# One cross-attention kernel, a second written-out order: the 2,366 steps rearranged, and the engine chosen anew where there is a choice

## The chip, the cores and the metric

The kernel runs on one core of one Trainium2 chip. Its engines run side by side, each through a list of instructions of its own, strictly in order: TensorE (PE, matrix products; loading its weights is listed apart as PEld), VectorE (DVE), ScalarE (ACT), GpSimd (POOL) and SyncE (SP, which here issues nearly all transfers). An instruction waits on semaphores for what it reads, and everything behind it on the same engine waits with it. The metric is device time in microseconds (us) of one execution; smaller is better.

## What is computed

Two batches of 2,048 tokens with 640 features (`x`) attend, in 8 heads of 80 features, to 124 text tokens, and the result gets an adapter term that is built from 4 further tokens (`ca`). Cut to what matters:

```python
query = x @ Wq;  keyt = enc @ Wk;  valt = enc @ Wv
hs = mha(query, keyt, valt)                            # softmax over 124 tokens
ca_q1 = einsum('btc,th->bch', ca, Wq_ca)[:, indices]   # 384 rows, repeated over 2048
ca_hs1 = mha(ca_q1, x, x)                              # softmax over 2048 tokens
ca_hs2 = mha(ca_hs1 @ Wq, ca @ Wk_ca, ca @ Wv_ca)      # softmax over 4 tokens
out = (hs + ca_hs2) @ Wout + b_out + x
```

All data are float32.

## The kernel before

**An order written out by hand of a planner.** The kernel consists of small tasks, Python generators that yield steps (`Do`: an engine or a choice of engines, what must be known before, which room is taken and freed). Nothing in the kernel decides the order. The string `ORDER` lists 2,366 entries; `Desk.run` takes them one by one, and each entry lets the task of that number do its next step. So the order of the entries of one engine is the order of that engine's instructions. A letter behind the number names the engine where a step has a choice (a ACT, v DVE, g POOL, n none); without a letter the first engine of the step's list is taken. Tasks are numbered as they are begun. The first 37 numbers are fixed (36 is the adapter of batch 0), then come the groups of the 16 units, then numbers that are given out as tasks start others.

**What the tasks do.** x comes in blocks of 512 tokens (`x_load`, turned by DVE), and each gives queries (`queries_fast`: a product by a scheme with 7 products of halves in place of 8, so with sums of halves of x and of Wq ahead of it, its strips of 32 columns in four parts of the array). The adapter of a batch (`adapter`) makes 24 blocks of scores of which DVE takes maxima (`mx`), then 24 blocks of which ACT takes exponentials (`ea`), each followed by a product that sums over tokens (`contract`, tile `acc`). After the last comes a chain that passes through all engines (`second`): `divide` (DVE), `less` (DVE, tiles `s2f`, `m`, `p`), an exponential (ACT), `share` (DVE, `r`, `p2t`), a product `pt_p` (PE, with `rows` made on POOL by `rows_of_tokens`), a copy, and a transfer to HBM from which each unit of the batch reads its part.

**Units.** The 32 tiles of 128 tokens are taken in 16 units of two. `text_scores` makes scores (`sc`), `softmax` takes maxima (DVE), exponentials (ACT), a scaling (POOL or DVE) and a turn (DVE); the result goes to HBM (`kept`) and comes back with keys along the partitions (`pT`). Then comes the hidden product (`ph`) and the output product (`po`). Seven units (0 to 4, 6 and 7) use sums of halves again (`text_out_fast`, four chains of products; between two products on one bank DVE adds the first to the rows of x: task `sums_chain`). The other nine (`text_out`) split both factors into a high part `top`, a rest `low` and a `mix` of both, and make 15 products in a faster type for each of four quarters (`out_part`). For that, Wout is split once for its five chunks (`wout_part`: `top`, `low`, a scaling, `mix`, a scaling). The parts `low` lie in a tile that is free only after both `contract` tasks of batch 1, and no `out_part` can start before all five chunks are done.

**Names and lines.** All matmuls run at line 221, nearly all other instructions at line 236, transfers at line 246. `Desk.run` is at line 181, `second` and `rows_of_tokens` stand below line 1640, `sums_chain` and `out_part` below line 2140, and `stored` writes a row of the output once its last sum is there.

Of the kernel before, what the change touches and what calls it, by code (L numbers as in the profile page):

```python
# [8 lines left out]
F32 = mybir.dt.float32  # L9
# [5 lines left out]
P = 128  # L15
# [52 lines left out]
class Desk:  # L68
# [7 lines left out]
    2 4 4 0 2 36 0 0 2 0 0 2 0 0 2 0 0 2 0 0 2 2 124 2 4 2 0 128a 0 2 0 6 6 6 2 125 4 6 130a 126 4 131a 127 4 4  # L76
    132a 6 133v 2 3 4 6 3a 2 15 3 6 3a 15 15 3 6 3v 3 7 7 8 8 7 8 11 7 7 15 0 8 135a 0 134a 7 5 8 7 7 15 9 7
    137a 6 1 138a 136v 14 8 12 15 7 7 7 139a 7 7 141v 140v 7 142a 9 15 143a 8 144 15 9 8 8 36 8 145 5 15 15 8 8
    9 10 8 9 5 146 5 9 147 15 14 36 15 15 148 6 9 9 9 14 14 14 14 9 14 9 14g 129 152a 151v 149a 12 150v 15 153 6
    6 9 36 14 129 15 14 36 16 14g 11 9 129 129 101 36 155 155 12 155 155 11a 36 157 11 9 12 9 156a 9 155 12 158  # L80
    158 159v 158 158 158 9 36 160 162v 18 12 36 163a 12 13 36 117 123 158 17 154 158 158 158 154 154 39 161 123
    17 117v 161 165g 154 161 117v 171 175 17 161 166g 161 164 18 164 164 17 18 117g 36 164 117g 154 154 164 117g
    164 161 18 176a 164 36 164g 161 16 36 18 18 167g 171 177 16 164 16 16 16 18 36 178a 117v 117 18 43 16 36 16g
    171 181 161 117g 18 18 180 164 168g 180 36 182a 16 17 180 117g 179 180 36 179 16 171 183 16g 174 185 184a 18
    180 18 180 18 36 172 186 36 174 18 17 17 179 18 179 174 188 170 187 187 19 20 21 161 21 187 187 172 192 187
    20 189 190 21 187 36 43 36 179 179 21 173 203 203 203 191 191 36 193 191 173 204 169 103 203 191 180 36 180g
    203 191 19 21 203 21 194g 180 36 19 200 209 20 21 195g 19 36 19 191 21 39 102 210a 191 19 21 21 36 19 191
    212 200 213 211 19g 205 211 212 17 196g 20 214a 203 19 212 197g 211 212 36 200 215 211 212 180 203g 201 212
    191 20 19 212 21 216a 21 19g 21 36 20 20 21 212g 211 211 21 206 217 217 36 22 23 24 24 202 24 200 218 217
    217 24 206 222 219a 203 217 36 22 223 24 217 203 36 24 47 22 22 22 208 228 226 202 202 22 24 207 229 24 44  # L90
    226 226 226 212 226 36 22 208 36 226 220 22g 24 207 230 202 224 208 232 199 198 105 202 231 212 226 36 23 24
    233 234g 47 36 20 226g 240 245 23 24 24 202 202 202 23 241 246a 22 241 241 40 241 36 235v 23 241 226 237g 22
    241 36 240 247 226 236g 154 23 23 248a 24 51 24 249 249 202 249 249 249 221 221 249 179 36 241 250 241g 221
    240 255 221 250 250 221 36 22g 244 257 256a 250 221 241 240 259 258a 250 36 241 221 244 154 36 250 55 260
    250 48 250g 36 221 261 242 261 261 24 261 36 25 26 27 27 244 262 239 261 27 261 243 26 264g 250 27 265g 36
    261 243 271 263 267g 27 36 242 273 238 107 179 250 266g 51 104 251 27 274 261g 36 272 270 279 26 36 23 253
    277 280a 27 227 275 270 281 227 275 275 154 261 275 179 275 277 283 282v 261 275 36 284a 278 285 36 221 225
    55 286v 179 225 275 227 275g 225 36 287 225 278 27 287 287 227 36 287 27 27 270 288 287 225 287 275 278 290
    269 276 289 275 287 36 36 36 36 287g 227 227 270 292 291 36 225 225 225 225 276 294 293 252 252 27 25 52 36
    295 287 252 154 252 59 25 252 25 211 26 296 296 296 252 27 296 27 296 59 106 27 296 27 36 28 29 29 30 287 26  # L100
    298 252 252 36g 298 252 296 299v 298 254 254 305 310 29 211 298 30 297 300g 298 36 30 56 36 311v 26 26 268
    26 109 296g 36 25 30 305 314 313 301g 312 30 36 315a 254 312 36 254 254 305 316 25 298 312 36 298 296 298g
    312 36 308 296 297 306 211 317a 312 30 313 36 313 313 312 25 36 305 320 30 308 322 321v 313 312 30 313 36 63
    302g 36 30 30 312 254 326 227 254 312 326 312 326 323 326 36 297 309 327 326 298 326 36 298 67 211 328 25 30
    297 30 227 312 254 36 329 309 36 30 329 60 30 312 329 30 312 309 330 304 326 329 31 32 326g 254 36 297 32
    331 312 227 36 318 326 324 31 329 312 227 329 326 36 319 319 31 312 10 36 319 67 33 33 33 31 340 31 312 36
    339 312 36 339 29 329 329g 339 312 339 36 332g 33 329 29 36 333g 33 312 339 312 340 334g 29 29 339 33 36 341
# [142 lines left out]
def kernel(  # L250
# [42 lines left out]
    desk = Desk(tc)  # L293
# [827 lines left out]
    def sums_of_wq():  # L1121
# [1245 lines left out]
```

## Time and profile before

| | |
|---|---|
| device time, median of 3 runs | 566.38 us |
| lowest and highest of them | 563.15 and 566.64 us |
| span of the profiled execution | 562.1 us |
| busy: PE, DVE, ACT, POOL | 549.2, 402.2, 276.3, 208.1 us |
| moved by transfers | 101.38 MB |

The span runs from the first to the last instruction; what an execution takes around it has no row of its own, and the three timed runs lie 1.1 to 4.5 us above the span. Durations in the following are those of the one profiled execution. A busy PE says that a product is under way, not that the next one could not have come sooner.

### The profile page before, as it was taken

How to read it: one execution, taken by the hardware profiler on the slowest of the kernel's cores; microseconds unless marked ns; L12 is line 12 of the kernel's file. 1: busy time of each engine (PE TensorE's matmuls, PEld its weight loads, DVE VectorE, ACT ScalarE, POOL GpSimd, SP SyncE). 2: the span in 40 equal slices, each digit the busy share in tenths (PEclk: the TensorE clock that was granted, in tenths of full speed). 3: DMA queues.
4: the chain of work that ended last, by engine and by line, in shares of the span. 5: the costliest groups of instructions: out<-in, count | busy, mean ns of one | idle time of the engine just before them, and what ended most of it. 6: DMA issues, size and time to landing. Idle time of an engine off the chain costs nothing.

```text
span 562.1 us, 17332 instructions
## 1 busy us (share of the span) xinstructions
PE 549.2 (98%) x7338; PEld 337.8 (60%) x7338; DVE 402.2 (72%) x621; ACT 276.3 (49%) x752; POOL 208.1 (37%) x206
## 2 busy tenths in 40 slices
PE   9999999999999999999999999999999899999997
PEld 8563455556555655455365445455554477989796
DVE  2457999999996564589999998655735886449542
ACT  3122645445338898886524524589878432111200
POOL 7002625344424522013559364512424830441040
PEclk9999999999999999999999999999999989999999
DMA  8994759774876899446558895859865367977533
GB/s 258 244 175 121 163 123 166 163 159 142 170 199 155 183 251 180 136 160 176 177 126 247 226 232 133 255 149 254 244 172 177 74 124 215 264 215 195 160 123 129
DMA packets 151549, 101.38 MB, mean 180 GB/s; under 512 B 86476, under 2 KB 130012, under 8 KB 151472
## 3 DMA queue, kind: packets, MB, share of 16 engines
q1 hardware_dynamic: 150704, 99.88, 69.5%
q8 instruction: 58, 0.95, 0.8%
q0 software_dynamic: 768, 0.40, 0.4%
q14 instruction: 19, 0.16, 0.1%
HBM read 61.34 MB, written 38.90 MB: 178 GB/s over the span
## 4 chain that ended last, share of the span: by engine, by line
PE 82%; DVE 7%; DMA 5%; ACT 2%; issue 2%; SPq 1%; DVEq 0%; ACTq 0%
PE po L221 23%; PE pq L221 23%; PE acc L221 7%; PE sc L221 6%; PE s L221 6%; PE ph L221 5%; PE pq_first L221 3%; PE pyz L221 3%; DVE mx L236 2%; ACT p L236 1%; DMA bias<-in_L_xattn_b_out_dram 1%; PE pk L221 1%; PE unread L225 1%; ACT ea L236 1%; PE pv L221 1%
## 5 line engine op out<-in xcount | busy, mean ns | idle before, releaser
L236 DVE TENSOR_REDUCE mx<-s 128x4 f32<-128x2048 f32 x48 | 109.2, 2275 | 2.9 <-PE s L221 2.8
L236 POOL TENSOR_TENSOR p<-p,r 128x992 f32<-128x992 f32 x29 | 53.8, 1856 | 141.1 <-DVE r L236 135.0
L236 ACT ACTIVATE ea<-s 128x2048 f32<-128x2048 f32 x48 | 90.4, 1884 | 25.6 <-PE s L221 25.3
L236 ACT ACTIVATE p<-sc,m 128x124 f32<-128x124 f32 x256 | 89.5, 374 | 25.7 <-DVE m L236 25.7
L236 ACT ACTIVATION_READ_ACCUMULATOR p<-sc,m 128x1 f32 x256 | 55.5, 217 | 0.0
L221 PE MATMUL pq<-xt,wq_sb 128*32 128x256 f32 x896 | 54.3, 381 | 0.6 <-DVE q L236 0.6
L236 DVE TENSOR_REDUCE m<-sc 128x4 f32<-128x496 f32 x64 | 40.6, 662 | 13.9 <-PE sc L221 13.7
L221 PE MATMUL acc<-ea,y_sb 128*32 128x384 f32 (+2 forms) x768 | 50.1, 383 | 0.0
L221 PE MATMUL ph<-pT,vpad 128*32 128x256 f32 x768 | 45.8, 380 | 0.8 <-DMA out_dram<-x_more 0.3
L236 DVE STREAM_TRANSPOSE eb<-p 128x1024 f32<-128x1024 f32 x32 | 39.5, 1233 | 4.5 <-POOL p L236 3.3
L221 PEld LDWEIGHTS pq<-xt,wq_sb 128*32 128x32 f32 x896 | 27.5, 110 | 22.9 <-issue 5.5
L221 PEld LDWEIGHTS sc<-kmain,q 64*128 64x128 f32 x512 | 31.8, 187 | 11.6 <-issue 8.4
L221 PE MATMUL pq<-xt,wq 128*32 128x512 f32 x320 | 38.8, 595 | 0.0
L221 PE MATMUL po<-wout_sums,hs 128*32 128x320 f32 x448 | 35.4, 438 | 3.5 <-DVE x_more L236 2.9
L221 PE MATMUL sc<-kmain,q 64*128 64x124 f32 x512 | 37.5, 283 | 0.1
L221 PE MATMUL po<-wout_sb,hs 128*32 128x320 f32 (+1 forms) x452 | 36.4, 434 | 0.7 <-DVE prod L236 0.6
L221 PE MATMUL po<-wout_low,ks 128*128 128x320 f32 x204 | 35.7, 308 | 0.0
L221 PEld LDWEIGHTS ph<-pT,vpad 128*32 128x32 f32 x768 | 24.4, 110 | 18.6 <-issue 2.6
L236 POOL TENSOR_TENSOR last_rows<-last_rows,bias 128x640 f32<-128x640 f32 x10 | 17.0, 1697 | 44.7 <-DMA last_rows<-in_x_dram 44.7
L221 PE MATMUL po<-wout_top,ks 128*128 128x320 f32 x180 | 32.5, 311 | 0.0
L221 PEld LDWEIGHTS acc<-ea,y_sb 128*32 128x32 f32 x768 | 21.1, 109 | 17.3 <-issue 8.6
L221 PEld LDWEIGHTS po<-wout_low,ks 128*128 128x128 f32 x204 | 31.3, 188 | 0.0
(232 smaller groups left out, 951.4 us busy)
## 6 DMA issues: line engine op xcount, KB each, us to landing
kept<-eb SPq DMA_DIRECT2D x32, 512.0 KB
pT<-kept SPq DMA_DIRECT2D x48, 256.0 KB
landing<-away SPq DMA_DIRECT2D x60, 128.0 KB
xi<-in_x_dram SPq DMA_DIRECT2D x28, 256.0 KB
x_more<-in_x_dram SPq DMA_DIRECT2D x17, 320.0 KB
out_dram<-x_more SPq DMA_DIRECT2D x16, 320.0 KB
last_rows<-in_x_dram SPq DMA_DIRECT2D x15, 320.0 KB
out_dram<-last_rows SPq DMA_DIRECT2D x14, 320.0 KB
```

Of the source, the lines that this page charges most:

```text
L221: self.pin(self.nc.tensor.matmul(out[strip], lhsT[:, strip], rhs, **kw))
L225: self.pin(self.nc.tensor.matmul(out, zeros, zeros, start=True, stop=True))
L236: return lambda *args, **kw: self.pin(getattr(engine, what)(*args, **kw))
```

## The change

It is all in the order, in the choice of engines, and in the bookkeeping that lets the order be made: a few rooms (tiles or banks that tasks share) are now freed or added by the step itself and no longer by the line behind it, the two steps of the hidden parts' `mix` became a helper that offers the same engines, and the stores of the output are tasks that exist from the start of a unit and wait for marks, where before the last sum started them. What is computed, and with which instructions, stays the same; of `BY_SUMS`, the tiles and the transfers nothing is changed. The entries were laid out anew with every transfer taken to land later than was estimated for what waits for it.

Both lists have 2,366 entries. Of the lists, the lines around the end of the second adapter and the last line stand here; with entries counted from 0, the first lines shown begin with entry 1965 before and 1947 after. In the part before, 515 is the second `contract` task of batch 1, 541 is `second`, 542 `rows_of_tokens`, 536, 537, 538, 543 and 544 are the five `wout_part` tasks. In the part after, the same are 542, 560, 561, and 543, 546, 549, 562, 563; 556 to 559 are the four chains of unit 4, 540 the end of a chain of unit 6, 129 the scores of unit 15, 70 unit 5, whose parts are 565, 566 and 567 and whose four output quarters are 568 to 571.

```diff
     ORDER = """
...
-    515 515 450 544v 544a 538v 538a 536v 536a 543g 543a 537v 99 116 120 451 538v 538a 543v 543a 541 533 533 60
-    84 11 84 84 84 537a 537v 541 541 541 60 547a 547 542 534 60 548a 548 548v 548 544g 544a 532 532 60 80 80
-    549a 549 549v 549 60 80 80 80 533 542 542 541 541a 541 84 119 92 80 88 88 88 88 88 88 547v 547 536g 536a 535
...
-    626 636 72 640 638 638 637 639 637 641 72 627 642 640 599 643 639 644 620 92 620 645
...
+    542 106 338 561 542 556 561 154 154 562 542 561 556 551v 556 542 542 480 546v 542 562 129 148 556 546 542 560 557
+    561 152 70 481 562 563 549v 560 560 560 70 556 565 70 561 549 540 76 563v 565 563 70 543v 566 563 565a 560 566 100
+    100 567 70 543 556 558 567 560 557 567a 562v 560 563 100 546v 557 562 549v 546 100 100 567v 549 559 543v 566 543
+    565v 556 64 558 152 566 569 540 151 100 556 106 547 557 568 564 564 564 564 571 564 100 112 112 112 112 112 47 112
...
+    120 626 118 641 635 642 626 119 132 125 108 640 88 642 643 90 633 130 640 89 633 131
     """
...
-        yield Do("NONE", lambda: None, ["late"], marks=["wq room"])
+        yield Do("NONE", lambda: None, ["late"], grows=[(halves[1], 1)], marks=["wq room"])
...
-        halves[1].grow(1)
...
-                op = yield Do("PE", scores, [("cop", b)], needs=[(quad, 1), (eas, 1)])
+                st = pieces(v)[-1][0]
+                ends_ = j == 1 and 512 * (v + 1) == CAD * (st + 1) and st % 4 == 3
+                op = yield Do(
+                    "PE", scores, [("cop", b)], needs=[(quad, 1), (eas, 1)],
+                    frees=(lambda st=st: [(zops, room_of["zop", b, st // 4])]) if ends_ else (),
+                )
...
-                    zops.give(room_of["zop", b, st // 4])
+                    late["ps_"]=0
...
+    def mixing(mix, top, low, after, marks):
+
+        def first():
+            if desk.engine == "ACT":
+                desk.a_activation(mix(), raw(low()), AF.Identity, scale=UP)
+            else:
+                mixed(mix(), raw(top()), raw(low()))
+
+        op = yield Do(("DVE", "ACT"), first, after)
+
+        def second():
+            if op.ran == "ACT":
+                minus(mix(), raw(top()), raw(mix()))
+
+        yield Do(("NONE", "POOL", "DVE"), second, marks=marks)
...
-    def stored(m, k, u, added):
+    def stored(m, k):
 
         b, st = tiles(m)[k]
...
+        for u in (2,) if m < UNITS - 1 else (0, 1):
+
+            def store(u=u):
+                cols = slice(*spans[u])
+                dma(out[b, st * P : (st + 1) * P, cols], xr_of[m][k][0][:, cols])
...
+            yield Do(
+                "SP", store, added,
+                frees=lambda: [(rows, xr_of[m][k][1])] if u == 2 else [],
+            )
```

The last entries tell which unit ends: before, entry 2365 is the store of unit 13, one of whole rows; after, it is the second store of unit 15 (131), one of half rows.

More of the change, by code (lines that the diff above doesn't have):

```diff
@@ L81 @@
[L81 to L95, printed above, removed]
@@ L2188, in add @@
                     desk.v_tensor_tensor(t, t, po[:, :HALF], ALU.add)
-                op = yield Do("DVE", add, [op.at], frees=[(banks, s)] if end else [])
+                op = yield Do(
+                    "DVE", add, [op.at], frees=[(banks, s)] if end else [], marks=[("added", m, i, n, k)],
+                )
                 at = [op.at]
-                key = (m, i, 2)
-                ends.setdefault(key, []).append(op.at)
-                if len(ends[key]) == 4:
-                    yield Fork(stored(*key, ends[key]))
         for n, steps in enumerate(chains):
@@ L2237, in hidden_parts @@
         )
-        def scaled():
-            if desk.engine == "ACT":
-                desk.a_activation(cols("mix"), cols("low", True), AF.Identity, scale=UP)
-            else:
-                mixed(cols("mix"), cols("top", True), cols("low", True))
-        op = yield Do(("DVE", "ACT"), scaled)
-        both = op.ran == "ACT"
-        yield Do(
-            ADDS if both else "NONE", lambda: both and minus(cols("mix"), cols("top", True), cols("mix", True)),
-            marks=[("hs mix", m, c0)],
-        )
+        yield from mixing(lambda: cols("mix"), lambda: cols("top"), lambda: cols("low"), [("hs low", m, c0)], [("hs mix", m, c0)])
     def out_part(m, i, u, hs):
@@ L2275, in add @@
             desk.v_scalar_tensor_tensor(t, po[:, :HALF], 1.0 + DOWN, t, ALU.mult, ALU.add)
-        op = yield Do("DVE", add, [op.at, ("xr", m, i)], frees=[(banks, s)])
-        key = (m, i, 2 if m < UNITS - 1 else u)
-        ends.setdefault(key, []).append(op.at)
-        if len(ends[key]) == (2 if key[2] == 2 else 1):
-            yield Fork(stored(*key, ends[key]))
-    ends = {}
+        yield Do("DVE", add, [op.at, ("xr", m, i)], frees=[(banks, s)], marks=[("added", m, i, u)])
     spans = (0, HALF), (HALF, H), (0, H)
-    def stored(m, k, u, added):
+    def stored(m, k):
         b, st = tiles(m)[k]
-        t, i, _ = xr_of[m][k]
-        cols = slice(*spans[u])
-        yield Do(
-            "SP", lambda: dma(out[b, st * P : (st + 1) * P, cols], t[:, cols]), added,
-            frees=[(rows, i)] if u == 2 else [],
-        )
+        for u in (2,) if m < UNITS - 1 else (0, 1):
+            def store(u=u):
+                cols = slice(*spans[u])
+                dma(out[b, st * P : (st + 1) * P, cols], xr_of[m][k][0][:, cols])
+            if m in BY_SUMS:
+                parts = (((0, 0), (0, 2), (2, 0), (3, 0)), ((0, 1), (0, 3), (1, 0), (1, 1)))[k]
+                added = [("added", m, k, *part) for part in parts]
+            else:
+                added = [("added", m, k, v) for v in ((0, 1) if u == 2 else (u,))]
+            yield Do(
+                "SP", store, added,
+                frees=lambda: [(rows, xr_of[m][k][1])] if u == 2 else [],
+            )
     blocks = [(b, sb) for b in range(B) for sb in range(NSB)]
@@ L2304, in text @@
         yield Fork(probabilities(m))
+        for k in range(2):
+            yield Fork(stored(m, k))
     begin = desk.begin
```

152 lines of the change are left out of this document (79 added, 73 removed).

## The prediction, made before the changed kernel was run

> **What bounds the kernel now.** I read the page's totals first, then the slices, then the waits of PE, then windows around the one place where the slices show a hole.
>
> ```profile
> span 562.1 us, 17332 instructions
> ...
> PE 549.2 (98%) x7338; PEld 337.8 (60%) x7338; DVE 402.2 (72%) x621; ACT 276.3 (49%) x752; POOL 208.1 (37%) x206
> ...
> PE   9999999999999999999999999999999899999997
> ...
> PEclk9999999999999999999999999999999989999999
> ...
> PE 82%; DVE 7%; DMA 5%; ACT 2%; issue 2%; SPq 1%; DVEq 0%; ACTq 0%
> ```
>
> PE is busy for 549.2 of 562.1 us, so its open idle time is 12.9 us in all. The chain that ended last gives only 82% to PE, which looks like more room. It isn't: where the chain names DVE or a transfer, the slices above still have PE at 9, so PE worked on something else while the step that came next was released. The waits show what PE itself lost, and to whom:
>
> ```profile
> PE po L221 <- DVE x_more L236: 2.9, 1, 2.9
> PE unread L225 <- DVE zeros L236: 1.1, 1, 1.1
> PE s L221 <- DVE mx L236: 1.1, 2, 0.8
> PE pt_p L221 <- DVE ks L236: 0.5, 1, 0.5
> PE ph L221 <- DMA out_dram<-x_more: 0.3, 1, 0.3
> ```
>
> The largest wait, 2.9 us, is on DVE and happens once. The one wait of PE that is put down to a transfer is 0.3 us. So the idea that the list is laid out by, a margin for late transfers, insures against something that costs this execution next to nothing in open waits. What a new order can win or lose is decided elsewhere: in the hole of slice 32. Its windows (columns: busy time of PE, PEld, DVE, ACT, POOL, then the granted clock) and its instructions:
>
> ```profile
> 438.98:456.64 17.66, 14.32 (x197) 7.51 (x196) 17.20 (x28) 8.38 (x15) 14.57 (x13) 0.90 0.32 65
> ...
> 446.00:447.00 1.00, 0.96 (x20) 0.31 (x12) 1.00 (x1) 0.68 (x1) 0.93 (x2) 1.00 0.00 0
> 447.00:448.00 1.00, 0.00 (x0) 0.00 (x0) 1.00 (x3) 0.76 (x2) 1.00 (x2) 1.00 0.20 12
> 448.00:449.00 1.00, 0.00 (x0) 0.00 (x0) 0.96 (x3) 0.60 (x1) 0.93 (x2) 1.00 0.94 174
> 449.00:450.00 1.00, 0.18 (x4) 0.16 (x8) 0.97 (x4) 0.60 (x2) 0.93 (x2) 1.00 0.67 174
> ...
> 451.00:452.00 1.00, 1.00 (x12) 0.21 (x4) 0.96 (x2) 0.55 (x2) 1.00 (x1) 0.50 1.05 231
> ```
>
> ```profile
> 438.43 0.55 PE L229 MATMUL pt_acc<-ident,accs 128*128 128x128 f32 x3
> ...
> 439.29 0.46 DVE L236 TENSOR_TENSOR prod<-pt_acc,r 128x288 f32<-128x288 f32 x1
> 439.66 5.51 DVE L236 TENSOR_TENSOR wout_low<-wout_sb,wout_top 128x640 fp32r<-128x640 f32 x4
> ...
> 440.40 1.28 PE L221 MATMUL po<-wout_sums,hs 128*32 128x320 f32 x16
> ...
> 441.50 1.05 PE L221 MATMUL ph<-pT,vpad 128*32 128x256 f32 x16
> ...
> 445.10 2.10 DVE L236 TENSOR_TENSOR wout_mix<-wout_top,wout_low 128x640 fp32r<-128x640 f32 x2
> ...
> 447.13 1.66 DVE L236 TENSOR_REDUCE s2f<-prod 128x24 f32<-128x192 f32 x3
> ...
> 449.29 0.47 DVE L236 TENSOR_TENSOR x_more<-x_more,po 128x320 f32<-128x320 f32 x1
> ...
> 449.82 1.66 PE L221 MATMUL po<-wout_sums,hs 128*32 128x320 f32 x16 [2.85 <-DVE x_more L236]
> ...
> 450.68 0.24 DVE L236 TENSOR_REDUCE r<-p 128x24 f32<-128x96 f32 x1
> ...
> 451.30 1.07 DVE L236 TENSOR_TENSOR p2t<-p,r 128x96 f32<-128x96 f32 x1
> 452.21 1.27 DVE L236 TENSOR_TENSOR ks<-ph,ks 128x512 fp32r<-128x512 f32 x2
> ...
> 453.04 1.52 PE L221 MATMUL pt_p<-rows,p2t 128*32 128x512 f32 x12 [0.49 <-DVE ks L236]
> ...
> 456.64 1.00 PE L221 MATMUL po<-wout_top,ks 128*128 128x320 f32 x5
> ```
>
> The last product of the adapter of batch 1 (`pt_acc`) ends at 438.98. From there to the first product of `out_part` at 456.64, DVE is busy for 17.20 of 17.66 us: it is the bound of this stretch, and PE has too little else to do. DVE takes four `wout_low` and two `wout_mix` first, then `s2f` and the rest of `second`, and only then the `x_more` sum that PE's next step waits for. PE is idle for 17.66 − 14.32 = 3.34 us. At once the granted clock falls to 0.50; the mean of 0.90 over the stretch is a loss of 0.10 × 17.66 = 1.8 us. The place costs 5.1 us.
>
> **The change, part by part.** *Bookkeeping* (rooms freed by the step, `mixing`, `stored`): no instruction more or less, on any engine; it costs nothing by itself, and what it lets the order do is counted below.
>
> *The end of the second adapter.* Read from the lists. Before, between `divide` (entry 1966) and `less` (1985) stand six of DVE's `wout_part` steps (544v, 538v, 536v, 537v; 538v, 543v), as in the trace. After, `less` (1973) comes right behind `divide` (1972), `share` at 1983, and `pt_p` at 2001. So the wait of `second` on DVE's splitting of Wout goes. What is late next? `out_part` (569, entry 2037), which needs all five chunks split and the three parts of unit 5. DVE's steps from 1972 to 2031 are, with the durations of the rows above: the division 0.7 (0.46 and a reciprocal, together from 439.0), `less` 2.2 (447.13 to 449.37), `share` 1.6 (450.68 to 452.37, its reciprocal between), three `wout_low` 5.51 / 4 = 1.38 each, 4.1, four `wout_mix` at 1.08 (below), 4.3, the three `low` parts of unit 5 1.7 (1.27 for two and some 0.4 for the half-size one), its three `mix` steps about 1.7 by the same row, and two sums of chains 0.9. That is 17.2 us, as long as before (17.20), for it is the same work: one `wout_low` moved ahead of `divide` (546v, entry 1965), and one `wout_mix` more is on DVE (four, not three).
>
> ```profile
> L236 DVE TENSOR_TENSOR wout_mix<-wout_top,wout_low 128x640 fp32r<-128x640 f32 x3 | 3.2, 1084 | 0.0
> ...
> 376.83 1.49 PE sc L221 x24
> ```
>
> PE's steps in the same stretch after are: scores of unit 15 (entry 1968) 1.5, `ph` of unit 5 three times 1.05, 3.2, `pt_p` 1.5 (at the slow clock, so at most), and seven steps of chains (557, 556, 540, 558, 557, 559, 556), two with 8, four with 12 and one with 4 matmuls at 1.28 / 16 = 0.08 each, 5.4. Sum 11.6 us. Before, PE's work there was 14.32 less the 1.8 that the clock cost, 12.5. So 0.9 us less cover stands over a stretch of equal length: the hole moves from ahead of `x_more`'s user to ahead of `out_part` and doesn't shrink. I take **+0.9 us**. Bounds: if other work that PE has later is pulled in and the hole goes with its clock loss, −5.1; if the hole is one piece as before and DVE's steps wait for each other, a second time the 1.8 us of clock and 1.5 us more, +3.3.
>
> *The clock there.* Idle from 446.96 to 449.82, 2.86 us, was enough here for the half clock, as the 0.50 shows. In a sentence of its own: the Trainium skill, "TensorE: Matmul & The Clock Gate", Part 1, has the clock fall after an idle window of about 3.4 us; by that rule a hole cut into pieces under 3.4 us would save the 1.8, but this trace has it fall after 2.86, so I keep the loss.
>
> *The tail.* The kernel ends with the store of the unit that comes last.
>
> ```profile
> 558.10 0.49 DVE L236 SCALAR_TENSOR_TENSOR x_more<-po,x_more 128x320 f32<-128x320 f32 x1 [1.69 <-PE po L221]
> 558.62 0.33 SPq L246 DMA_DIRECT2D out_dram<-x_more  x1
> ```
>
> Before, that is unit 13 with a whole row of 320 KB, and from its issue at 558.62 to the end of the span are 3.5 us. After, unit 15 is last, in half rows. Half the bytes save between nothing and half of the 3.5, 1.7; most of a short transfer is not its bytes, so I take **−0.6 us**.
>
> *The small waits.* All other open waits of PE behind the start are on DVE or ACT, none above 0.8 us. A new order has its own. I take **−1.1 us**, the two waits on `mx`, the largest of a kind that a list laid out by durations should see; bounds −3 and +3, about all of them gone or doubled.
>
> *The margin itself.* The new list shows no clear distance that grew. From the last part of a unit's `pT` to its first hidden product it has at least 14 entries (unit 3, 1607 to 1621) and for most units 20 to 60; before, 19 to 78, with one at 1 (unit 4) whose product waited for nothing that the trace shows. I cost it at nothing: transfers lie beside PE's products, and the one wait above is 0.3.
>
> Sum: +0.9 − 0.6 − 1.1 = −0.8 us on the profiled 562.1. The runs' median is 566.38, 4.3 above that span, so I put the forecast at 566.4 − 0.8 = **565.6 us**. That is no change: a measurement of this kernel can tell about 1%, 5.7 us.
>
> **The rivals.** *The hole is filled (faster).* If PE's work of later units runs in the stretch where DVE splits Wout, the 5.1 us go, and with the tail's and a few small waits' 2 it is 7 us: **559**. For it: in the new list tops of Wout start as early as entry 1843 (before 1925), so planning reached farther ahead. Against: the two sums above.
>
> *The plan finds time that the busy share hides (much faster).* A busy PE need not be fed at its rate.
>
> ```profile
> 158.00:165.80 7.80, 7.80 (x144) 4.50 (x144) 7.30 (x14) 3.00 (x17) 3.02 (x2) 1.00 0.85 213
> ```
>
> If PE had the room that the weight loads suggest, some 3% would be easy: **549**. Against: this row is 144 strips back to back, nothing between them, and weight loads are busy for 4.50 of 7.80 (58%), as much as over the whole span (60%). The Trainium skill, "Trainium Kernel Development and Optimization", Performance Expectations, calls matmul busy time a bad measure and the weight loads' busy share a good one. By that rule 40% of PE would be open; the row shows 42% "open" where the array has no gap, since loads of four strips overlap.
>
> *DVE becomes the bound of the first half (slower).* From 56 to 168 us DVE has nearly nothing left:
>
> ```profile
> 56.00:168.00 112.00, 111.14 (x1696) 59.99 (x1690) 106.75 (x131) 54.27 (x208) 48.41 (x38) 1.00 0.73 161
> ...
> L236 ACT COPY q<-pq 128x512 f32<-128x512 f32 x20 | 11.8, 591 | 24.5 <-PE pq L221 24.5
> ...
> L236 DVE COPY q<-pq 128x512 f32<-128x512 f32 x8 | 5.5, 687 | 4.9 <-PE pq L221 4.9
> ```
>
> It is busy for 106.75 of 112, so 5.2 us are free. The 20 copies of queries that ACT does would cost DVE 0.69 each; from the eighth that moves there, DVE decides, and all 20 would cost 13.7 − 5.2 = 8.5 us: **575**. Against: in its first 1,200 entries the new list names DVE 27 times by letter, the old one 28 times.
>
> *A unit's `pT` comes late (slower).* If unit 3's 14 entries are too few (562.1 / 2366 = 0.24 us each on the mean, 3.3 us), and the five units with 21 to 29 wait too, at 1 to 2 us each, it is some 8 us: **574**. Against: engines run ahead of the list, and transfers did not hold PE before.
>
> **How the numbers follow.** No change, 0.50. The hole filled 0.24 and hidden time 0.05, so faster 0.29. DVE as the bound 0.12 and late `pT` 0.09, so slower 0.21. The likeliest case by itself, with its bounds, reaches from 560 to 572. For 8 in 10 I go beyond the filled hole, short of the hidden time, and up to the two slower cases: 555 to 574.
>
> **What would show it.** Right: PE idle of 3 to 6 us between the adapter's last `pt_acc` and the first `po<-wout_top`, now ahead of that product, DVE above 95% busy there, the clock once at 0.50; `pt_p` 6 to 9 us behind `pt_acc` (14.1 before); the end within 3.5 us of the last store's issue. Wrong: a stretch between the two that is shorter than 15 us, a DVE share of the first half that differs by more than 5 us, waits of `ph` on `pT<-kept`, or a PE total that moves by more than 5 us with the same 7,338 matmuls.

## The result, and the profile after

| | before | changed | ratio, 95% interval |
|---|---|---|---|
| device time, median of 13 runs each | 565.66 us | 562.50 us | 0.9939, 0.9921 to 0.9957 |
| lowest run | 563.15 us | 560.18 us | |
| span of the profiled execution | 562.1 us | 561.4 us | |

The changed kernel is 0.6% faster. That lies within the 1% that the prediction called no change, at 562.5 where 565.6 was forecast. But the interval is clear of 1: these runs tell differences well below 1%, and the gain is real. Three executions of before, at 729.54, 839.28 and 1,373.79 us, are left out of all ratios and means.

The two profiled executions understate the difference. In every run that lists both, the time lies 1.7 to 1.9 us above the span. So the profiled execution of before took some 563.9 us, 1.8 below its kernel's median of 565.66, and that of the changed kernel took 563.07, 0.6 above its own. Together that is 2.4 of the 2.5 us by which the medians' difference, 3.2, exceeds the spans', 0.7.

The totals, the slices of PE and of its clock, and the head of the chain, from the changed kernel's page (its matmuls stand at L216, with L220 and L224 for the `unread` products and for turns such as `pt_acc`, which were L225 and L229 before; nearly all else is at L231):

```profile
span 561.4 us, 17345 instructions
...
PE 549.2 (98%) x7350; PEld 337.9 (60%) x7350; DVE 406.2 (72%) x637; ACT 276.8 (49%) x749; POOL 180.4 (32%) x194
...
PE   9999999999999999999998999999999999999997
...
PEclk9999999999999999999999999999999999999999
...
PE 78%; DVE 11%; SPq 4%; ACT 3%; issue 2%; DMA 2%; DVEq 0%; ACTq 0%
```

PE's busy time is the same as before to the tenth; DVE has 4.0 us more and POOL 27.7 us less. The dip of slice 32 is gone, from PE's row and from its clock. What PE waited for, in us in all, times and longest, from the changed kernel's waits:

```profile
PE s L216 <- DVE mx L231: 2.2, 5, 0.8
PE s L216 <- ACT ea L231: 1.3, 5, 0.5
PE unread L220 <- DVE zeros L231: 1.1, 1, 1.1
...
PE ph L216 <- DMA pT<-kept: 0.5, 1, 0.5
```

The wait of 2.9 us on `x_more` isn't there any more. The waits of `s` on `mx` grew from 1.1 us in 2 to 2.2 us in 5. Now the place of the hole, from the last `pt_acc` of batch 1 to the first product of `out_part`, in the changed kernel's windows (busy time of PE, PEld, DVE, ACT, POOL, then the granted clock):

```profile
442.51:456.69 14.18, 14.18 (x220) 8.52 (x220) 13.97 (x28) 9.99 (x19) 7.11 (x8) 1.00 0.34 73
```

The stretch took 17.66 us before; it takes 14.18 now. PE has no gap in it, its clock stays at 1.00, and DVE needs 13.97 us for 28 instructions where it needed 17.20 for 28. So DVE's sum there, which the prediction held to be fixed work, shrank by 3.2 us. The groups of both kernels in the stretch tell why (times, busy us, mean ns of one). Before:

```profile
L236 DVE TENSOR_TENSOR wout_low<-wout_sb,wout_top 128x640 fp32r<-128x640 f32 x4 | 5.5, 1437 | 0.0
L236 DVE TENSOR_TENSOR p2t<-p,r 128x96 f32<-128x96 f32 x1 | 1.1, 1069 | 0.0
```

Changed:

```profile
L231 DVE TENSOR_TENSOR wout_low<-wout_sb,wout_top 128x640 fp32r<-128x640 f32 x3 | 3.0, 1008 | 0.0
L231 DVE TENSOR_TENSOR wout_mix<-wout_top,wout_low 128x640 fp32r<-128x640 f32 x3 | 2.3, 817 | 0.0
L231 DVE TENSOR_TENSOR p2t<-p,r 128x96 f32<-128x96 f32 x1 | 0.3, 334 | 0.0
```

The same step takes 1,437 ns on the mean before and 1,008 now; `p2t` takes 1,069 and 334; `wout_mix`, 1,084 in the prediction's row, takes 817. In the old stretch POOL is busy for 14.57 of 17.66 us, mostly with the selects of `rows` and with its own splitting of Wout; now for 7.11 of 14.18. The shorter stretch also holds 23 matmuls more than the old one (220, before 197), so the hole was filled with work that PE did elsewhere before.

On the profiled executions, by the clock of the trace: `pt_acc` ends 3.53 us later than before (442.51 against 438.98), the stretch is 3.48 us shorter, and from the first `out_part` product, at 456.69 and 456.64, to the end it is 0.8 us less. That makes the 0.7 us between the spans. So the new order arrives at the second adapter late, and its shorter stretch makes this good. The same four windows of the first 434 us, added up; the first row is of before, the second of the changed kernel:

```profile
sum 434.00, PE 428.81 PEld 236.25 DVE 324.28 ACT 251.44 POOL 168.04; mean PE 107.20 PEld 59.06 DVE 81.07 ACT 62.86 POOL 42.01
```

```profile
sum 434.00, PE 426.15 PEld 234.48 DVE 323.55 ACT 249.50 POOL 153.20; mean PE 106.54 PEld 58.62 DVE 80.89 ACT 62.37 POOL 38.30
```

By 434 us, PE was busy for 2.66 us less in the new order. The first block of scores `s` starts later too, at 45.26 us before; in the changed kernel:

```profile
49.01 0.51 PE L216 MATMUL s<-zop,cop 32*128 32x512 f32 x4 [0.65 <-DVE q L231]
```

These are single executions, and they differ among themselves. The run with one move, below, has the steps of before in their old order up to entry 1,967, and in its profiled execution the same sum is

```profile
sum 434.00, PE 425.75 PEld 234.40 DVE 320.63 ACT 247.65 POOL 163.91; mean PE 106.44 PEld 58.60 DVE 80.16 ACT 61.91 POOL 40.98
```

Over the eight profiled kernels that begin with the old order for some 425 us or more, the sum goes from 425.27 to 429.10 us, so 2.66 alone would prove nothing. What is clear of that spread is smaller: from 56 to 168 us PE is busy for 110.66 us in the changed kernel and for 111.01 to 111.14 in the eight, from 168 to 294 us for 124.55 and for 124.94 to 125.00. That the new first part costs time rests on the times of the second experiment.

### The profile page after: what moved, and what is told of

Its sections match the earlier page's. It is cut to its first block, busy times and chain, and to the rows that moved or that the text cites. A ratio compares the mean times of both kernels' runs of the same rounds, so it can differ in the third digit from the quotient of the medians.

```text
span 561.4 us, 17345 instructions
## 1 busy us (share of the span) xinstructions
PE 549.2 (98%) x7350; PEld 337.9 (60%) x7350; DVE 406.2 (72%) x637; ACT 276.8 (49%) x749; POOL 180.4 (32%) x194
## 4 chain that ended last, share of the span: by engine, by line
PE 78%; DVE 11%; SPq 4%; ACT 3%; issue 2%; DMA 2%; DVEq 0%; ACTq 0%
PE po L216 25%; PE pq L216 17%; PE ph L216 7%; PE acc L216 6%; PE s L216 6%; PE sc L216 6%; DVE mx L231 5%; SPq L241 4%; PE pq_first L216 3%; PE pyz L216 2%; ACT ea L231 2%; PE pk L216 1%; PE unread L220 1%; DVE xt L231 1%; DVE m L231 1%
## 5 line engine op out<-in xcount | busy, mean ns | idle before, releaser
L231 DVE TENSOR_REDUCE mx<-s 128x4 f32<-128x2048 f32 x48 | 109.3, 2276 | 3.0 <-PE s L216 2.6
L231 ACT ACTIVATE p<-sc,m 128x124 f32<-128x124 f32 x256 | 90.0, 374 | 34.9 <-DVE m L231 34.9
L231 ACT ACTIVATE ea<-s 128x2048 f32<-128x2048 f32 x48 | 90.5, 1885 | 20.7 <-PE s L216 20.5
L231 POOL TENSOR_TENSOR p<-p,r 128x992 f32<-128x992 f32 x22 | 40.9, 1860 | 116.2 <-DVE r L231 100.5
L231 ACT ACTIVATION_READ_ACCUMULATOR p<-sc,m 128x1 f32 x256 | 55.4, 216 | 0.0
L216 PE MATMUL pq<-xt,wq_sb 128*32 128x256 f32 x896 | 54.1, 381 | 0.2 <-ACT p L231 0.2
L216 PE MATMUL acc<-ea,y_sb 128*32 128x384 f32 (+2 forms) x768 | 49.9, 383 | 0.0
L231 DVE TENSOR_REDUCE m<-sc 128x4 f32<-128x496 f32 x64 | 40.6, 660 | 11.4 <-PE sc L216 11.3
L216 PE MATMUL ph<-pT,vpad 128*32 128x256 f32 x768 | 45.6, 381 | 0.5 <-DMA pT<-kept 0.5
L231 DVE STREAM_TRANSPOSE eb<-p 128x1024 f32<-128x1024 f32 x32 | 39.5, 1233 | 5.2 <-DMA kept<-eb 2.7
L216 PEld LDWEIGHTS pq<-xt,wq_sb 128*32 128x32 f32 x896 | 28.0, 110 | 21.7 <-issue 4.4
L216 PE MATMUL pq<-xt,wq 128*32 128x512 f32 (+1 forms) x308 | 39.0, 596 | 0.0
L216 PEld LDWEIGHTS sc<-kmain,q 64*128 64x128 f32 x512 | 31.9, 187 | 11.8 <-issue 9.2
L216 PE MATMUL sc<-kmain,q 64*128 64x124 f32 x512 | 37.8, 284 | 0.1
L216 PE MATMUL po<-wout_sb,hs 128*32 128x320 f32 (+1 forms) x452 | 36.1, 433 | 0.0
L216 PE MATMUL po<-wout_low,ks 128*128 128x320 f32 x204 | 35.7, 308 | 0.0
L216 PEld LDWEIGHTS ph<-pT,vpad 128*32 128x32 f32 x768 | 23.8, 110 | 18.7 <-issue 2.5
L216 PE MATMUL po<-wout_sums,hs 128*32 128x320 f32 x448 | 34.6, 435 | 0.3 <-DVE last_rows L231 0.3
L216 PE MATMUL po<-wout_top,ks 128*128 128x320 f32 x180 | 32.5, 310 | 0.0
L216 PEld LDWEIGHTS acc<-ea,y_sb 128*32 128x32 f32 x768 | 21.2, 109 | 18.3 <-issue 9.7
L231 POOL TENSOR_TENSOR x_more<-x_more,bias 128x640 f32<-128x640 f32 x13 | 20.6, 1586 | 33.6 <-DMA x_more<-in_x_dram 33.6
L216 PEld LDWEIGHTS po<-wout_low,ks 128*128 128x128 f32 x204 | 31.3, 188 | 0.0
```

The lines of the kernel that those rows point to most:

```text
L216: self.pin(self.nc.tensor.matmul(out[strip], lhsT[:, strip], rhs, **kw))
L231: return lambda *args, **kw: self.pin(getattr(engine, what)(*args, **kw))
```

## The experiments

All kernels of this section are made on the changed kernel's code, with another list of entries. The list of most of them is two lines longer, so that its L218 and L233 are L216 and L231 of the changed kernel. A join is a list that takes the steps of one list's first part in the other list's order, on the other list's engines. "Before" in their ratios was run again beside each group of them. Theory A, at first: the gain comes from the end of the second adapter, where the new order keeps DVE's splitting of Wout apart from what the adapter's end needs, and the first part of the new order gives some of it back.

**The old order on the changed code.** All of the list is that of before, engines included; the numbers differ, since the tasks are numbered anew.

```diff
     ORDER = """
-    0 36 0 2 4 4 2 0 2 0 2 0 2 0 0 2 0 2 0 2 0 2 0 2 0 156 2 0 4 2 0 160 6 0 6 6 4 6 162v 158 0 157 4 159 4 163 5 6
+    2 4 4 0 2 36 0 0 2 0 0 2 0 0 2 0 0 2 0 0 2 2 156 2 4 2 0 160a 0 2 0 6 6 6 2 157 4 6 162a 158 4 163a 159 4 4 164a 6
...
```

> The old order of all steps and the old engines, written for the changed code: only the bookkeeping of the change (rooms freed by the steps, the helper for the mix, the stores as tasks) is left. If the order alone makes the 0.6%, this takes the time of before: ratio 0.998 to 1.002, with the hole ahead of 449.8 us of 3 us or so and a half clock behind it. If the bookkeeping brings something by itself (a tile or a bank taken in another turn), the ratio is 0.994 to 0.997.

Measured: 565.18 us, ratio 1.0004 (0.9980 to 1.0029). The waits of PE have the hole as before:

```profile
PE po L218 <- DVE x_more L233: 2.9, 1, 2.9
```

So the bookkeeping by itself does nothing that the interval would show, and the difference is in the list. Its stretch from `pt_acc` to `out_part` takes 17.21 us.

**The old order up to 425 us, the new one behind.** The steps of the new list's first 1,876 entries stand in the old order; the join is in the middle of this line.

```diff
...
+    338 538 58 530 64 64 64 154 545g 530 112 59 11 441 539 70 64 441 338 539 538 154 544g 338 538 525 525v 129 338 540
...
```

> All steps that the new list has in its first 1,876 entries (to some 425 us) in the old order among themselves and with the old engines, everything behind in the new order. Theory A (the gain is made around the end of the second adapter, by a stretch between the last pt_acc and the first product of out_part that took 17.7 us before and 14.2 us after; the first part of the new order gives some back): PE has no idle time over 1 us there, the stretch takes 14 to 15 us, and the time is below both kernels, ratio to before 0.988 to 0.993. Theory B (the first 425 us of the new order are what is better, and the hole only moves elsewhere when the order ahead of it is the old one): ratio 0.998 to 1.002.

Measured: 558.31 us, ratio 0.9892 (0.9866 to 0.9918), faster than both kernels; the interval lies below that of the changed kernel. Its stretch, in its windows, and its first 434 us:

```profile
437.28:451.46 14.18, 14.18 (x220) 8.52 (x220) 13.97 (x28) 9.97 (x19) 7.08 (x8) 1.00 0.35 74
...
sum 434.00, PE 429.01 PEld 235.84 DVE 322.20 ACT 252.65 POOL 166.22; mean PE 107.25 PEld 58.96 DVE 80.55 ACT 63.16 POOL 41.56
```

The short stretch of the new order (14.18) and the first part of the old one (429.01 us of PE's work, against 428.81 and 426.15): both stand in one kernel. By the middles of the intervals, 0.9892 against 0.9939, the new order's first part costs some 2.7 us.

**The mirror: the new order up to 425 us, the old one behind.**

```diff
...
+    532 542 542 509 532 112 441 529 529g 70 529 538 545v 539 338 542 538 129 546 546 338 338 542 542 539 539 338 338
...
```

> The mirror of it: the new order for its first 1,876 entries, the old order and the old engines for all that is behind. Theory A: the hole of about 3 us and the half clock are back, and the time is at or over that of before, ratio 1.000 to 1.006. Theory B: the time of the new order, ratio 0.992 to 0.996.

Measured: 578.42 us, ratio 1.0238 (1.0211 to 1.0265), slower than either theory had it. The hole of 2.9 us is back, and there is a wait that neither kernel has:

```profile
PE sc L218 <- DVE x_more L233: 6.0, 1, 6.0
PE po L218 <- DVE x_more L233: 2.9, 1, 2.9
```

The 6.0 us are a seam where the lists meet: before the sum that these scores wait for, DVE itself stands still for 5.5 us until a transfer (`kept`) lets it write the tile `eb` again. This run shows the hole and no clean price for the rest.

**The old order, only the splitting of Wout on the new engines.**

```diff
...
-    562 562a 562 106 151 118 100 112 112 112 112 112 112 567v 567n 557g 557a 556 556 555 65 116 116 566 566 566 566
-    553 64 553 545 561v 558g 572 573 572 573 571 571 570 570 71 554 66 76 152 100 106 106 100 577a 577 577v 577n 106
+    562 562a 562 106 151 118 100 112 112 112 112 112 112 567v 567n 557v 557a 556 556 555 65 116 116 566 566 566 566
+    553 64 553 545 561v 558a 572 573 572 573 571 571 570 570 71 554 66 76 152 100 106 106 100 577a 577 577v 577n 106
...
```

> The old order throughout; of the engines only those of the steps that split Wout are the new ones, so that one mix goes from POOL to DVE, one scaling from POOL to ACT, and POOL has two steps of 1.8 to 2.1 us less beside DVE in the stretch from 439 to 457 us. Theory A1 (DVE's steps there are slow because POOL works at the same time; p2t took 1.07 us beside POOL and 0.33 us without): p2t at 0.33 us, wout_mix on DVE at 0.8 us, the stretch of 17.7 us shorter by 1 to 3 us though DVE has one step more, ratio 0.995 to 0.999. Theory A2 (the order of DVE's steps makes the hole, with second behind the splitting of Wout): the stretch is as long as before or longer by the added 0.8 us, ratio 0.999 to 1.003.

Measured: 565.65 us, ratio 1.0007 (0.9986 to 1.0027). POOL's busy time in the stretch falls from 14.57 to 10.68 us, and the hole stays:

```profile
439.19:456.48 17.29, 14.43 (x196) 7.64 (x196) 17.05 (x28) 7.98 (x15) 10.68 (x11) 0.90 0.32 67
```

One part of theory A1 came true. The POOL step beside which `p2t` had stood is gone, and `p2t` takes a third of the 1.07 us of before:

```profile
451.50 0.33 DVE L233 TENSOR_TENSOR p2t<-p,r 128x96 f32<-128x96 f32 x1
```

But the four `wout_low` ahead of it, which stand beside POOL's selects and a `wout_mix` as before, still take 5.51 us. These engines alone aren't the cause.

**Order and engines apart.** First the new order with each step on its old engine, then the old order with each step on its new one, over the whole list. A line of the first edit, and one of the second:

```diff
...
-    164 2 4 3 165v 4 3v 3 6 15 3v 2 6 7 7 3 7 15 3 7 7 3 8 15 7 167 166 7 7 7 168 7 7 169 170 7 171v 7 172 7 173v 7
+    164a 2 4 3 165v 4 3a 3 6 15 3a 2 6 7 7 3 7 15 3v 7 7 3 8 15 7 167a 166a 7 7 7 168v 7 7 169a 170a 7 171a 7 172v 7
...
-    165v 2 3 4 6 3a 2 15 3 6 3a 15 15 3 6 3v 3 7 7 8 8 7 8 11 7 7 15 0 8 167a 0 166a 7 5 8 7 7 15 9 7 169a 6 1 170a
+    165v 2 3 4 6 3v 2 15 3 6 3v 15 15 3 6 3a 3 7 7 8 8 7 8 11 7 7 15 0 8 167a 0 166a 7 5 8 7 7 15 9 7 169a 6 1 170a
...
```

> The changed kernel's order, with each step on the engine that it had before, where the step allows it. Theory A (the order alone brings the gain): ratio 0.992 to 0.997, and the stretch from the last pt_acc to the first out_part product at 14 to 15.5 us. Rival (the new engines are needed to fill the hole): the stretch at 16.5 us or more, ratio 0.999 to 1.008. A change that is worth less than 0.2% either way can't be told apart.

> The order of before, with each step on the engine that the changed kernel gives it. Theory A: ratio 0.999 to 1.006, the stretch at 16.5 us or more with the hole of about 3 us ahead of x_more's user. Rival (engines): ratio 0.990 to 0.996, no hole over 1 us.

Measured: 569.09 us, ratio 1.0054 (1.0030 to 1.0078), and 598.31 us, ratio 1.0579 (1.0540 to 1.0619), the second outside all that was expected. Theory A fails in the form that it had: the new order with the old engines is slower than before, though its stretch, 16.43 us, is a little shorter. The second kernel shows what a step can cost on another engine's in-order queue. Its waits and a row of DVE's timeline:

```profile
PE po L218 <- DVE ks L233: 14.6, 2, 11.2
...
550.22 0.83 DVE L233 TENSOR_TENSOR last_rows<-last_rows,bias 128x640 f32<-128x640 f32 x1 [4.37 <-DMA last_rows<-in_x_dram]
```

DVE waits 4.37 us for rows from memory to add the bias to them, and behind that step stand the splittings of `ks` that PE needs. Over the whole list, neither the new order nor the new engines win anything without the other.

**The old order with one move.** The steps of `wout_part` on DVE and ACT that stand between `divide` and `less` go behind `share`.

```diff
...
-    563 530 112 541 541 549g 59 538 538 538 538 563 538 551g 553 552v 553 538 538 538 480 565v 565a 559v 559a 557v
-    557a 564g 564a 558v 129 148 152 481 559v 559a 564v 564a 562 554 554 70 106 11 106 106 106 558a 558v 562 562 562 70
+    563 530 112 541 541 549g 59 538 538 538 538 563 538 551g 553 552v 553 538 538 538 480 129 148 152 481 562 554 554
+    70 106 11 106 106 106 558g 558v 562 562 562 565v 565a 559v 559a 557v 557a 564g 564a 558v 559v 559a 564v 564a 70
...
```

> The order and engines of before, with one move: the steps of wout_part on DVE and ACT that stand between divide and less of batch 1 go behind share, so that less stands directly behind divide. Theory S (DVE's sum of 17.2 us in the stretch is fixed work, as the prediction had it): the stretch stays at 16.8 to 18 us, PE idles 2.5 to 4 us in it, ratio 0.998 to 1.004. Theory M (DVE's steps are long because POOL's selects and splitting run beside two-tensor steps, so that another mixture of the same steps is shorter, and PE has work to do): the stretch at 14.5 to 16 us, DVE busy under 16, ratio 0.993 to 0.997.

Measured: 566.41 us, ratio 1.0021 (0.9997 to 1.0044), the stretch 18.57 us in the profiled execution, which was the slowest of 12, 4.4 us above their median. The edit did more than was announced: the `low` step of chunk 1 (558) came to POOL and its next step to DVE, and a `low` step of POOL (564g) went behind `share` with the rest. The wait on `x_more` is gone, and this one stands in its place, as the waits and the windows show:

```profile
PE pt_p L218 <- POOL rows L233: 3.9, 1, 3.9
...
443.46:462.03 18.57, 14.67 (x197) 8.59 (x197) 16.48 (x28) 7.75 (x14) 14.93 (x14) 0.91 0.31 65
```

POOL's timeline has the reason:

```profile
450.08 2.04 POOL L233 TENSOR_TENSOR wout_mix<-wout_top,wout_low 128x640 fp32r<-128x640 f32 x1 [2.72 <-ACT wout_low L233]
452.06 0.67 POOL L233 MEMSET rows<- 128x684 f32 x1
```

POOL stands still for 2.72 us ahead of a `wout_mix` whose input was moved back, and the masks `rows` that `pt_p` needs stand behind it in POOL's queue. Theory M's numbers didn't come; theory S has the ratio right, but its stretch is too short, and DVE, busy for 16.48 of 18.57 us, isn't the bound here. The run settles neither. It shows that bringing `less` forward isn't enough: a list moved on one engine can make a wait on the next.

**The old order for the start.** The steps of the new list's first 240 entries in the old order.

```diff
...
+    149g 149g 186 186 18 18 18 18 18 18 196 196 149g 36 196 17 196 196 193 18 193 193 197v 208a 36 193 18 16 198g 193
...
```

> The changed kernel with the old order for the steps that the new order has as its first 240 (to just behind the first block of scores), the new order behind. Theory L (what the first part of the new order gives back is the later start of the scores, 45.3 to 49.0 us, and nothing behind it): ratio 0.987 to 0.991, the first block of scores at 45 to 46 us. Rival R (it is spread over the first 425 us by DVE's longer work): ratio 0.993 to 0.996, and what is won at the start is lost again by 300 us (last pq at 298 instead of 295).

Measured: 570.95 us, ratio 1.0093 (1.0064 to 1.0122), outside what both expected. Again a seam, at 78 us:

```profile
PE sc L218 <- ACT rests L233: 7.7, 1, 7.7
```

The first scores come at 45.4 us, as wanted, and the last query product starts at 306.3 us, 298.6 without the 7.7, where the changed kernel has 298.8 and before 295.0. An early start of the scores by itself isn't kept, as rival R had it; with such a seam this is a hint and no proof.

**The join of 425 us with the old engines throughout; the same with only the splitting of Wout on the old ones.** Both are edits of the second experiment's list, at some 60 and at 3 entries.

```diff
...
-    561 152 70 481 562a 563a 549v 560 560 560 70 556 565a 70 561 549a 541 76 563v 565 563a 70 545v 566a 563g 565a 560
+    561 152 70 481 562a 563v 549v 560 560 560 70 556 565a 70 561 549a 541 76 563v 565 563a 70 545v 566a 563g 565v 560
...
```

```diff
...
-    561 152 70 481 562a 563a 549v 560 560 560 70 556 565a 70 561 549a 541 76 563v 565 563a 70 545v 566a 563g 565a 560
-    566 100 100 567a 70 545a 556 558 567 560a 557 567a 562v 560 563a 100 546v 557 562a 549v 546a 100 100 567v 549a 559
-    545v 566v 545a 565v 556 64 558 152 566n 569 541 151 100 556 106 547 557 568 564 564 564 564 571 564 100 112 112
+    561 152 70 481 562a 563v 549v 560 560 560 70 556 565a 70 561 549a 541 76 563v 565 563a 70 545v 566a 563g 565a 560
+    566 100 100 567a 70 545a 556 558 567 560a 557 567a 562v 560 563a 100 546v 557 562a 549v 546g 100 100 567v 549a 559
+    545g 566v 545a 565v 556 64 558 152 566n 569 541 151 100 556 106 547 557 568 564 564 564 564 571 564 100 112 112
...
```

> The join of experiment e2 (old order for the first 1,876 entries' steps, new order behind: ratio 0.989), with the engines of before throughout, so that only the order of the last part is new. Theory P (order and engines are a pair: the new order needs its engines, as e5 at 1.005 with the old ones and e6 at 1.058 with only the new ones suggest): ratio 0.995 to 1.003, the stretch from the last pt_acc to the first out_part product at 16 us or more. Rival O (the order of the end brings the gain, and what e5 lost it lost in the first 425 us, where its engines didn't fit either): ratio 0.988 to 0.992 and the stretch under 15 us.

> The join of e2 (ratio 0.989) with only the steps of wout_part on the engines of before (three steps: a top from ACT to DVE, a mix from DVE to POOL, a scale from ACT to POOL); the other 57 letters of the new part stay new. Theory W (those three are what e9 lost, 0.997 against 0.989, because they put 0.93 us of top on DVE and some 4 us on POOL beside DVE's steps): ratio 0.994 to 0.998, the stretch at 15.5 us or more. Rival H (it was the sums and scalings of the hidden parts, such as the 2.03 us on ks beside POOL's mix): ratio 0.988 to 0.992, the stretch under 15 us.

Measured: 564.14 us, ratio 0.9968 (0.9948 to 0.9987), stretch 18.10 us (in an execution that was the slowest of 12, 3.1 us above their median); and 560.74 us, ratio 0.9917 (0.9899 to 0.9935), stretch 14.49 us. So the engines of the last part are worth about two thirds of the second experiment's gain, by the middles of the intervals (0.0076 of 0.0108). The splitting of Wout is at most a smaller part of that: 0.0025, with intervals that overlap. What the larger part is can be read from the first kernel's waits and DVE's timeline:

```profile
PE po L218 <- DVE ks L233: 2.0, 1, 2.0
...
448.40 0.81 DVE L233 TENSOR_TENSOR wout_low<-wout_sb,wout_top 128x640 fp32r<-128x640 f32 x1
449.14 2.03 DVE L233 SCALAR_TENSOR_TENSOR ks<-ks 128x512 fp32r<-128x512 f32 x1
451.09 0.68 DVE L233 TENSOR_TENSOR ks<-ph,ks 128x512 fp32r<-128x512 f32 x1
```

and POOL's beside it:

```profile
448.74 1.88 POOL L233 TENSOR_TENSOR wout_mix<-wout_top,wout_low 128x640 fp32r<-128x640 f32 x1 [1.76 <-ACT wout_low L233]
```

The `mix` step of `ks` (565a, which becomes 565v) starts on DVE 0.4 us after POOL's `wout_mix`, ends 0.55 us after POOL's end at 450.62, and takes 2.03 us; a step of the same form takes 0.68 in the changed kernel (at 454.99). PE waits 2.02 us for the step behind it. In the second kernel, POOL has the same `wout_mix` for 1.90 us at 448.34, but the step's first half, a scaling, is on ACT and takes 0.62 (the subtraction follows on DVE later, at 454.18):

```profile
448.64 0.62 ACT L233 ACTIVATE ks<-ks 128x512 fp32r<-128x512 f32 x1
```

There is no wait then. The two stretches differ by 3.6 us, of which the wait is 2.0 and the half clock behind it, 0.09 of 18.10, is 1.6. So the choice of engine that counts here seems to be the one that takes a DVE step out of POOL's way. No run moved this step alone; 57 letters lie between the two kernels.

**Two other joins of old and new**, at the new list's entry 1,200 (about 285 us) and at 1,940, ahead of which the two lists have nearly the same steps.

```diff
...
+    151 403g 11 82 417 32 28 338 384 384 415 376 376 376 28g 338 406 421 35 31 10 415 415 415 376 378 338 82 418 338
...
```

```diff
...
+    124 338 338 154 557g 154 558v 154 78 545g 441 542 538 538 530 112 549g 59 538 11 106 559v 551g 106 338 106 552g
...
```

> The old order for the steps that the new order has as its first 1,200 (to about 285 us), the new one behind; the two lists nearly agree on which steps lie ahead of this cut, so that the join has no seam like that of e3 and e8. What the new order gives back (e2 0.989 against 0.994 of the changed kernel): if it lies ahead of 285 us (theory F), ratio 0.988 to 0.991; if it lies between 285 and 425 us (rival G), 0.993 to 0.996; if it is spread evenly, 0.991 to 0.993.

> As e2, with the cut at the new order's entry 1,940 in place of 1,876, where the two lists agree better on what lies ahead of it. If e2's gain comes from the end of the second adapter (theory A): ratio 0.987 to 0.992 again, the stretch at 14 to 14.5 us without a hole over 1 us. If part of it came from steps between 1,876 and 1,940 (the early tops of Wout and the part of low ahead of the adapter's end): 0.992 to 0.997 and a stretch over 15 us.

Measured: 561.41 us, ratio 0.9921 (0.9896 to 0.9946), and 559.81 us, ratio 0.9909 (0.9890 to 0.9927). The second agrees with the second experiment: nothing of the new order ahead of entry 1,940 is needed for the gain, and its stretch has no gap either.

```profile
438.93:453.38 14.45, 14.45 (x221) 8.61 (x221) 14.09 (x28) 9.71 (x19) 9.25 (x9) 1.00 0.33 68
```

The first lies between the changed kernel (0.9939) and the second experiment (0.9892). By the middles, the new order gives back some 1.0 us up to 285 us and 1.6 us from there to 425 us. As the intervals overlap, that it is spread over both parts is likely and not shown.

## Why the prediction was right or wrong

The forecast of no change held, and by luck: the term for the hole had the wrong sign, and a loss that it hadn't priced took back part of what that term missed. The sum had −0.8 us. The medians moved by −3.2. One of its own signs of being wrong came, a stretch shorter than 15 us, and in a small way another, one wait of `ph` on `pT<-kept`. Of its signs of being right, PE's idle time ahead of `out_part` and the half clock didn't come; DVE's share of the stretch, the place of `pt_p` and the tail did.

- **The step that failed** is "the hole moves from ahead of `x_more`'s user to ahead of `out_part` and doesn't shrink", at +0.9 us. The hole closed: the stretch went from 17.66 to 14.18 us, −3.48, without a gap and with 23 matmuls more in it. Two terms under it were off. DVE's work in the stretch was summed to 17.2 us with durations from the old stretch, where DVE's steps stood beside POOL's; in the new mixture the same kinds of step took 13.97. The largest differences are three `wout_low` (3.0 for 4.1), four mixes (3.1 for 4.3) and `p2t` (0.33 for 1.07). And PE's cover was summed to 11.6 us; it measured 14.18, so it grew by 1.7 us over the 12.5 of before and did not shrink by 0.9. The seven chain steps were counted as 68 matmuls, 5.4 us. The rows have 136:

```profile
L216 PE MATMUL po<-wout_sb,hs 128*32 128x320 f32 x56 | 4.4, 432 | 0.0
L216 PE MATMUL po<-wout_sums,hs 128*32 128x320 f32 x48 | 3.8, 434 | 0.0
...
L216 PE MATMUL po<-wout_sb,wout_sums 128*32 128x320 f32 x32 | 2.8, 432 | 0.0
```

  (Matmul records overlap, so the busy times of all groups add up to more than the stretch.) That was a miscount by a factor of two.
- The bound of −5.1 for this term was right to be there, and the rival that the hole is filled, with a stretch without a gap, is what happened at that place. It had 0.24. Its 559 us came only with the old first part ahead of it, 558.31 in the second experiment.
- **Not priced at all** was that the new order's first part could lose time: some 2.7 us, by the second experiment's ratio against the changed kernel's. The prediction looked for a bound there (DVE) and not for small losses. DVE's busy time from 56 to 168 us rose from 106.75 to this:

```profile
56.00:168.00 112.00, 110.66 (x1676) 59.73 (x1680) 108.45 (x136) 54.40 (x211) 42.86 (x35) 1.00 0.70 160
```

  That is 3.55 us short of the window, so DVE didn't become the bound. Between the two traces PE lost 0.48 us there, and 0.82, 0.40 and 0.95 in the other three windows; 0.82 and 0.95 lie within the spread of single executions.
- The small waits were taken at −1.1 us by the two waits on `mx` going. They went to five, 2.2 us. All listed waits of PE outside the old hole come to 5.1 us before and 7.9 after, so the term measured +2.8 in these two executions; the bounds of ±3 held.
- The clock was right as a fact of the row: 2.86 us of idle gave the half clock in this execution of the old order, and the changed kernel, without a gap, has none in the stretch. The loss of 1.8 us that the sum kept was gone with it.
- The tail gave −0.3 us, not −0.6: the last store is issued at 558.24 of 561.4, 3.2 us from the end where it was 3.5. Half the bytes took nearly as long here.

```profile
558.24 0.33 SPq L241 DMA_DIRECT2D out_dram<-x_more  x1
```

- The place of `pt_p` was right: it starts 7.8 us behind the end of `pt_acc` (442.51), with 6 to 9 forecast.

```profile
450.31 1.07 PE L216 MATMUL pt_p<-rows,p2t 128*32 128x512 f32 x12
```

- Late `pT`, the slower rival: 0.5 us in one wait. It didn't decide. Neither did the hidden time that the weight loads' share suggests: they are busy for 60% in all, and the best join won 1.1%.

What stays open: which steps of the first 425 us lose the 2.7 us; why PE is busy for the same 549.2 us in both traces, though 1.8 us of the old ones were half clock; whether one engine letter alone would bring what the 57 between the two joins with old engines bring; and how much of the 1.054 to 1.062 of the old order with the new engines lies outside the end of the kernel.

## What to carry to other kernels

A step's duration in a profile belongs to what ran beside it: before summing an engine's work in a new order, compare the same step alone and beside its neighbour, and price with the row that fits the new neighbours. A new order is to be judged by stages. Stages of two single traces can mislead, as the 425 to 429 us of one and the same first part show; a join of the two orders, timed over several runs, tells what a stage is worth, and here the join of the better halves gave more than either. Order and choice of engines are one plan, and half of it can be worse than none of it.

## What the runs showed of the hardware

**Some steps of DVE and POOL hold each other up, for whole instructions.** In the changed kernel's timelines of DVE and of POOL stand

```profile
445.72 0.81 DVE L231 TENSOR_TENSOR wout_low<-wout_sb,wout_top 128x640 fp32r<-128x640 f32 x1
...
447.25 1.40 DVE L231 TENSOR_TENSOR wout_low<-wout_sb,wout_top 128x640 fp32r<-128x640 f32 x1
```

```profile
445.64 0.67 POOL L231 MEMSET rows<- 128x679 f32 x1
446.38 1.60 POOL L231 TENSOR_SCALAR_AFFINE_SELECT rows<-rows 128x679 f32<-128x679 f32 x2
```

The same step takes 0.81 us beside a memset and 1.40 beside a select, ending 0.67 us after POOL's end at 447.98. The `mix` step of `ks` above began beside POOL's `wout_mix` and ended only 0.55 us after it. POOL is held up likewise. Of two pairs of selects in the kernel before, the first ran beside two `wout_mix` of DVE, the second beside DVE's reductions and short steps:

```profile
445.17 2.65 POOL L236 TENSOR_SCALAR_AFFINE_SELECT rows<-rows 128x684 f32<-128x684 f32 x2
...
448.50 1.59 POOL L236 TENSOR_SCALAR_AFFINE_SELECT rows<-rows 128x679 f32<-128x679 f32 x2
```

A DVE step with one operand in a bank of PSUM, in the kernel with only the splitting on its old engines, ran in the middle of the same `wout_mix` (448.34 to 450.24) without delay:

```profile
448.78 0.69 DVE L233 TENSOR_TENSOR ks<-ph,ks 128x512 fp32r<-128x512 f32 x1
```

The Trainium skill, "SBUF — State Buffer", section "SBUF: two separate sides", has it that a DVE operation with two SBUF inputs and a GpSimd operation that reads SBUF exclude each other for the whole instruction. The rows above agree, with 2.03 us for a step that takes 0.68 alone. One pair of this case doesn't: in the kernel with only the splitting on its old engines, POOL scales `wout_mix` from 452.15 to 454.47, and inside that time, at 453.57, DVE's step `ks<-ks,ks` of the same form takes its usual 0.68 us. The profile's spans on POOL are rough, so this is a hint and no proof.

**The same idle time can cost the clock or not.** Two kernels have the same gap of PE at the same place, 2.02 us in the join with the old engines and 2.04 us in the new order with the old engines. Behind it, the first kernel's windows of 1 us have

```profile
452.00:453.00 1.00, 1.00 (x16) 0.39 (x12) 1.00 (x4) 0.00 (x0) 0.00 (x0) 0.88 0.98 149
453.00:454.00 1.00, 1.00 (x12) 0.43 (x8) 1.00 (x3) 0.00 (x1) 0.00 (x0) 0.50 0.99 141
454.00:455.00 1.00, 1.00 (x12) 0.43 (x8) 1.00 (x2) 0.73 (x1) 0.21 (x1) 0.50 0.96 281
```

and the second's

```profile
455.00:456.00 1.00, 1.00 (x24) 0.45 (x16) 1.00 (x3) 0.00 (x0) 0.00 (x0) 1.00 0.99 148
456.00:457.00 1.00, 1.00 (x20) 0.46 (x16) 1.00 (x3) 0.74 (x1) 0.01 (x1) 1.00 0.93 274
```

with 24 matmuls in a microsecond at full clock against 12 at half. Their stretches are 18.10 and 16.43 us. The old hole had the same in its own executions: of the 71 of before that were timed beside the experiments, eight have a mean granted clock of 1.000 and the lowest 0.993, where 1.8 us lost in 562 make 0.997. (Whether the hole was there in each of them, their times don't tell.) So in these runs an idle time of 2 to 3 us was a chance of the half clock, and the price of such a gap is to be carried as two cases. The Trainium skill, "TensorE: Matmul & The Clock Gate", Part 1, has the clock fall after at least one idle window of about 3.4 us, in a window that runs freely. Here it fell after 2.02 us of idle time, and the measurement decides.
